# A graph network on one core: fixed places for the list's steps, PSUM places of their own for groups and dense blocks, and five count buffers

## The chip, the cores and the metric

The kernel runs on one core of one Trainium2 chip. The core has a matrix engine (PE, TensorE), a vector engine (DVE), a scalar engine (ACT), a general engine (POOL) and a queue engine (SP); each executes its own instructions strictly in order, and they wait for one another through semaphores. PE writes only into PSUM, which here is eight places ("banks") of 128 partitions x 2 KB, 512 float32 each. Everything else lies in SBUF (on the core) or DRAM, and DMA queues carry data between these.

The metric is device time in microseconds, median of the runs. The profile is one further execution, recorded by the hardware.

## The reference

The input is a graph of N = 12500 nodes with D = 256 features each and E = 200000 edges `src -> dst`, sorted by `dst`. The reference computes, first, three layers of mean aggregation, then a residual and a layer norm:

```
deg     = segment_sum(ones, dst)
inv_deg = 1 / max(deg, 1)
layer(h): agg = segment_sum(h[src], dst);  h @ W_self + (agg * inv_deg) @ W_neigh + b
h = relu(layer(x)); h = relu(layer(h)); h = layer(h)
x = layernorm(x + h)
```

and then an attention step over the same edges (4 heads of 16: scores of projected nodes, a softmax over each node's incoming edges, weighted sums, a few products with a 256 x 256 matrix), a residual and a layer norm. The attention step is not touched by the change.

## The kernel before

**Groups.** An aggregation is made as matrix products. 1792 edges (14 columns of 128) form a group. POOL gathers the sources' rows with 14 indirect DMAs (L121) into one of three buffers `xg`. DVE makes a one-hot of 128 x 1792 (L477, `oh`): for each edge, which of 128 consecutive nodes is its target; it compares the edges' relative targets with `nodes`, the numbers 0 to 127, which lie in a PSUM bank of their own (`gconst`, made at L471 by `group_consts`). PE multiplies the one-hot with the rows and sums in the bank `pA` (L906 in layer 1, L903 in layers 2 and 3), and carries over what the group before had begun (L486). In layers 2 and 3 a row is split in a high part (ACT, L895) and the low rest (DVE, L897), tile `hl` with two buffers of half a group; in layer 1 the rows go in as they are. Then a group's sums become means (ACT, L926), own rows `hb` and means are transposed on PE into `pT` (L384, function `turned`) and copied out to `hT` (DVE, L389); four products with the weights go into `pO` (L375, `sage_products`); DVE adds the bias in place (L365), ACT applies the relu (L367) and writes high parts (L682), DVE the low parts (`hs`, L684). In layer 3, DVE instead adds `x` (L369) and normalises, and `finish` transposes the result into `pT` once more (copied to `zT`, L389) and projects it into `pO` (L395, copied to `zu`, L397).

**Dense blocks.** The last 20 (layer 1) or 32 (layers 2 and 3) blocks of 128 nodes are not gathered. For these the kernel builds a table of counts, how often each node is a source for each target, as bytes in DRAM. A dense sweep goes over all 98 blocks of source nodes: it loads counts (`c8`) and rows in high and low parts (`hz`, three buffers in layers 2 and 3), casts the counts to float (`c32`, ACT, L772; five buffers in layer 1, three in layers 2 and 3), and sums on PE into `px` (L778; in layers 2 and 3 four banks, eight matmuls per source block). At a sweep's end its blocks pass through `end_block` (L723 on): the own rows `hbd` are transposed into `pT` (`hTd`, L389), products go into `pO` (L737) and, under the name pT, `pn` (L739), ACT copies one (`own`, L743), DVE joins both (L744), then come the same bias add and `finish`. All but the last sweep of a layer end in the banks `pT` and `pO` that the groups use; the last one ends in the `px` banks, through a small class `Spare`.

**The list.** In layer 1 the counts are formed besides: in eight parts of four blocks each. `row_ends` (L558 on) finds where each node's edges end, from a one-hot `oh16` made with the same `nodes` and summed by PE into `pO` (L563, read at L565). For each part, `load_edges` (L585 on) issues three loads on ACT's queue (`lim` L591, `prior` and `iv` L596), DVE turns them into first edges `org` and inverse degrees (L598 to L603), POOL gathers the sources and targets of these edges (`el`), and DVE makes keys of them (L613 to L630), which PE transposes (L634) and ACT copies (`kt`, L635). `form` then compares keys, four at a time (DVE, `oa` L656 and `ob` L657), PE multiplies the comparisons into `pc` (L665), ACT writes the counts (`win`, L668), and every finished block goes to DRAM (`cnt_d`, L673). The steps of the next part's `load_edges` are interleaved with `form` at fixed fractions of a part.

**PSUM.** The banks are `gconst`, `pT`, `pO` and `pA`, one each, and four for the rest: in layer 1 two `px` and two `pc`, in layers 2 and 3 four `px`.

**The order of the work.** The program is written as Python generators: per round three groups in different stages (late, far, now) take turns with units of a dense sweep and of the list. `chained` strings together PE's units (the first matmul of a unit behind the last of the unit before); `after` orders two instructions without a wait between engines. Apart from these, a scheduler places each instruction in its engine's order, by data and by a tile's buffers; two users of one PSUM bank are kept apart by waits.

Of the kernel before, what the change touches and what calls it, by code (L numbers as in the profile page):

```python
# [9 lines left out]
F32 = mybir.dt.float32  # L10
F32R = mybir.dt.float32r
# [6 lines left out]
OP = mybir.AluOpType  # L18
# [5 lines left out]
P = 128  # L24
# [24 lines left out]
def tile_gnn_resnorm(  # L49
# [341 lines left out]

    def project(ps, zT, zu):

        pz = ps.tile([zT.shape[2], KR], F32, name="pO")
        mm = [nc.tensor.matmul(pz, zT[:, c], uall[:, c].rearrange("p k r -> p (k r)"),  # L395
                               start=c == 0, stop=c == DC - 1) for c in range(DC)]
        return nc.vector.tensor_copy(zu, pz), mm[0], mm[-1]  # L397
# [90 lines left out]
    def fast_sage():  # L488
        with ExitStack() as fx:
# [11 lines left out]
            nc.vector.memset(top, 0.0)  # L501
            ones16 = wp.tile([P, 1], BF16, name="ones16")
            nc.vector.memset(ones16, 1.0)
            nodes = group_consts(cps)


            rows2 = rel.rearrange("p g j -> p (g j)")
# [50 lines left out]
            def row_ends(pool, g):  # L558

                oh = onehot(pool, nodes, mrel[:, g], BF16, "oh16", OP.is_le, 1)  # L560
                pn = ps.tile([1, P], F32, name="pO")
                for j in range(GT):
                    nc.tensor.matmul(pn, ones16, oh[:, j], start=j == 0, stop=j == GT - 1)  # L563
# [6 lines left out]
            held, whole, chain, closed, compared = [], [], [None], [None], [None]  # L570
            last = None

            def chained(first, last):
# [11 lines left out]
            def load_edges(pool, u):  # L585

                nonlocal last
                assert counted[0] >= needs[u]
                at = N0 + u * SG0 * P
                lim = pool.tile([P, 1], F32, name="lim")  # L590
                nc.scalar.dma_start(lim, ends_d[at - 1:at - 1 + SG0 * P, :].rearrange("(i t) o -> i (t o)", t=NC)[:, 0:1])  # L591

                iv = invd[:, u * SG0:(u + 1) * SG0]
                prior = pool.tile([P, SG0], F32, name="prior")
                for t, a in ((prior, at - 1), (iv, at)):
                    nc.scalar.dma_start(t, ends_d[a:a + SG0 * P, :].rearrange("(d p) o -> p (d o)", p=P))  # L596
                yield
                nc.vector.tensor_scalar_min(lim, lim, float(E - SL))  # L598
                org = pool.tile([P, 1], I32, name="org")
                nc.vector.tensor_copy(org, lim)  # L600
                nc.vector.tensor_sub(iv, iv, prior)
                nc.vector.tensor_scalar_max(iv, iv, 1.0)
                nc.vector.reciprocal(iv, iv)  # L603
                yield
                el = pool.tile([P, 2, SL], I32, name="el")
                for i, t in enumerate((sources, ends)):
                    i = gather(el[:, i], t, org)
                    if last is not None:
                        after(last, i)
                    last = i  # L610
                yield
                lead = pool.tile([P, 1], F32, name="lead")
                nc.vector.tensor_scalar(lead, pidx, float(NC), float(at), op0=OP.mult, op1=OP.add)  # L613
                part = pool.tile([P, 2, SL], I32, name="part")
                first = nc.vector.tensor_scalar(part[:, 0], el[:, 0], P - 1, None, op0=OP.bitwise_and)
                if compared[0] is not None:
                    after(compared[0], first)
                nc.vector.tensor_scalar(part[:, 1], el[:, 0], 7, None, op0=OP.logical_shift_right)
                keys = pool.tile([P, 4, SL], F32, name="keys")
                nc.vector.tensor_copy(keys[:, :2], part)  # L620

                node, odd, ok = keys[:, 3], keys[:, 2], part.bitcast(F32)[:, 0]
                nc.vector.tensor_scalar(node, el[:, 1], lead, None, op0=OP.subtract)
                nc.vector.tensor_scalar(odd, node, 2.0, None, op0=OP.is_ge)
                nc.vector.scalar_tensor_tensor(keys[:, 1], keys[:, 1], 2.0, odd, op0=OP.mult, op1=OP.add)
                nc.vector.scalar_tensor_tensor(odd, odd, -2.0, node, op0=OP.mult, op1=OP.add)
                nc.vector.tensor_scalar(odd, odd, 255.0, 1.0, op0=OP.mult, op1=OP.add)
                nc.vector.tensor_scalar(ok, node, 0.0, None, op0=OP.is_ge)
                nc.vector.scalar_tensor_tensor(ok, node, float(NC), ok, op0=OP.is_lt, op1=OP.mult)
                nc.vector.scalar_tensor_tensor(keys[:, 1], keys[:, 1], 1.0, ok, op0=OP.add, op1=OP.mult)  # L630
                kt = pool.tile([P, 3, P], F32, name="kt", bufs=2)
                pt = ps.tile([P, 3, P], F32, name="pT")
                for i in range(3):
                    nc.tensor.transpose(pt[:, i], keys[:, i], ident)  # L634
                nc.scalar.activation(kt, pt, AF.Copy)  # L635
                held.append(kt)

            def form(pool, psum):
# [6 lines left out]
                for i, u in enumerate(parts):  # L645
# [1 line left out]
                    kt = held.pop(0)  # L647
                    ahead = load_edges(pool, parts[i + 1]) if i + 1 < NU else iter(())
                    for i0 in range(0, P, CP):
                        if i0 in (0, P // 4, P // 4 * 3):  # L650
                            next(ahead, None)
                        oa = pool.tile([P, CP, P], BF16, name="oa", bufs=2)
                        ob = pool.tile([P, CP, NQ * 2], BF16, name="ob", bufs=2)
# [5 lines left out]
                        for c in range(0, CP, 2):  # L659
                            d = (i0 + c) * NC % P  # L660
                            if d == 0:
# [3 lines left out]
                            mm = [nc.tensor.matmul(pc[:, i].rearrange("p b t -> p (b t)"), oa[:, c + i], ob[:, c + i],  # L665
                                                   start=True, stop=True) for i in range(2)]
                            chained(*mm)
                            nc.scalar.activation(  # L668
                                win[:, :, d:d + 2 * NC].bitcast(U16).rearrange("p b (i t) -> p b i t", t=2),
                                pc.rearrange("p i b t -> p b i t"), AF.Copy)  # L670
                            if d + 2 * NC == P:
# [29 lines left out]
            class Spare:  # L701
# [3 lines left out]
                    self.pool, self.i = pool, i  # L705

                def tile(self, shape, dt, name):
                    return self.pool.tile(shape, dt, name=f"px{('pT', 'pO').index(name)}{self.i}")

            def sweeps(l, dk, dps, lk):  # L710

# [9 lines left out]
                def end_block(k, d, aggT, bank):  # L721
# [39 lines left out]
                for k0 in range(ND - NDL[l], ND, sg):  # L761
                    assert all(k in whole for k in range(k0, k0 + sg))
                    px = [[dps.tile([P, 512], F32, name=f"px{f}{i}") for i in range(sc // 512)] for f in range(DC)]
                    for b in range(NQ):
# [7 lines left out]
                        nc.scalar.activation(c32.rearrange("p (k d) -> p k d", d=P), c8[:, :, b % CB], AF.Copy)  # L772
                        made = []
                        for f in range(DC):
# [45 lines left out]
            for l in range(L):  # L820
# [6 lines left out]
                with ExitStack() as lx:  # L827
                    done, formed = 0, 0
                    lk = lx.enter_context(tc.tile_pool(name="layer", bufs=2))
                    dk = lx.enter_context(tc.tile_pool(name="dense", bufs=2))  # L830
                    dps = lx.enter_context(tc.tile_pool(name="dense_ps", bufs=1, space=PSUM))
                    steps_ = sweeps(l, dk, dps, lk)
                    if l == 0:
                        tk = lx.enter_context(tc.tile_pool(name="tabs", bufs=1))
# [4 lines left out]
                    def group(g):  # L839
# [40 lines left out]
                        pa = ps.tile([P, 2 * D], F32, name="pA")  # L880
                        for a in (0, H):
                            if a and final:
                                hT, *mm = turned(wk, ps, [hb], "hTd")
                                chained(*mm)
                                po = ps.tile([P, D], F32, name="pO")
# [63 lines left out]
                        store_rows(tiles, at[0], made, at[1])  # L949
# [369 lines left out]
```

## Time and profile before

| | us |
|---|---|
| median of 9 runs (lowest, highest) | 7903.2 (7852.78, 7944.66) |
| the profiled execution | 7867.0 |
| its span | 7865.2 |
| PE busy, share of the span | 5523.6, 70% |
| DVE busy | 3769.2, 48% |
| ACT busy | 3346.1, 43% |
| POOL busy | 4785.6, 61% |

The mean granted clock of PE is 0.776 of full speed. The profile's page lists the busy time of each engine, the busy share in 40 slices of the span, and the costliest groups of instructions; further views of the trace give the waits of an engine by what ended them, the same counts for a stretch of time, and single instructions in order of time. Layer 1 lies from the start to about 2080 us, layer 2 to 3765, layer 3 to 5550, and the attention step after that. In such lines "PE px L778 <- ACT c L772" means that PE stood idle before an instruction of line 778, which writes `px`, until ACT had finished one of line 772, which writes `c`; "issue" means that nothing in the trace shows what was waited for, "remote" that a signal from elsewhere came late, SPq, ACTq are DMA queues. Names in lines leave off figures at their end (`c` stands for `c32` and for `c8`).

### The profile page before, as it was taken

The page shows a single profiled execution, that of the slowest core. Times are in us where ns is not written, and L with a number is a line of the kernel's source. Part 1 is how long each engine was busy: PE and PEld are TensorE (multiplying, and loading weights), DVE is VectorE, ACT ScalarE, POOL GpSimd, SP SyncE. Part 2 cuts the span into 40 slices and gives each one's busy share as a digit, 9 for nine tenths or more (in the row PEclk, how much of TensorE's full clock was granted, in tenths as well). Part 3 has the DMA queues.
Part 4 walks back from the last instruction along what each step waited for, and adds up shares of the span by engine and source line. Part 5 has one row for each costly group of instructions (what it writes and reads, how often), then busy time and mean ns, then how long its engine had stood idle before and what let it go on. Part 6 is the DMA issues. An engine that isn't in the chain of part 4 may idle for free.

```text
span 7865.2 us, 85868 instructions
## 1 busy us (share of the span) xinstructions
PE 5523.6 (70%) x23570; PEld 4420.8 (56%) x23570; DVE 3769.2 (48%) x9563; ACT 3346.1 (43%) x6092; POOL 4785.6 (61%) x4977
## 2 busy tenths in 40 slices
PE   4688888788588888888688888877444444444445
PEld 3566666667466666666476667665343443343344
DVE  4555444444233444444344545545455555555555
ACT  1333333334154555554344445444344444444444
POOL 5566665566566566665565556556466666666665
PEclk6799999899789999999798989988555555555555
DMA  7767777677466666776576767665233322222322
GB/s 197 245 226 242 238 250 245 222 244 254 151 214 208 215 216 216 224 224 191 169 221 206 214 199 219 211 191 175 88 92 91 91 86 91 92 85 91 91 86 68
DMA packets 896848, 1391.60 MB, mean 177 GB/s; under 512 B 191296, under 2 KB 540504, under 8 KB 892253
## 3 DMA queue, kind: packets, MB, share of 16 engines
q1 hardware_dynamic: 654927, 834.75, 32.6%
q0 software_dynamic: 213152, 496.65, 21.5%
q10 hardware_dynamic: 28270, 54.56, 2.0%
q8 instruction: 189, 3.10, 0.2%
q14 instruction: 310, 2.54, 0.1%
HBM read 1175.15 MB, written 210.33 MB: 176 GB/s over the span
## 4 chain that ended last, share of the span: by engine, by line
PE 32%; issue 10%; DVE 9%; another core or an unknown queue 6%; POOL 6%; DMA 3%; ACT 2%; DVEq 0%; ACTq 0%; POOLq 0%; SPq 0%
PE px L778 11%; POOL zs L121 5%; PE pA L903 4%; PE pD L1050 3%; PE pA L1078 3%; PE pO L375 2%; DMA zs<-zu_d,srcI 2%; PE pO L402 2%; DVE zz L1058 2%; PE pO L408 2%; DVE hl L897 1%; DVE lg L1061 1%; PE pT L384 1%; DVE wf L1067 1%
## 5 line engine op out<-in xcount | busy, mean ns | idle before, releaser
L121 POOL DMA_INDIRECT xg<-h_d,srcI x2128 | 2074.1, 975 | 1397.4 <-issue 617.4
L778 PE MATMUL px<-c,hz 128*128 128x512 f32 x8232 | 2400.1, 431 | 233.6 <-issue 134.5
L121 POOL DMA_INDIRECT zs<-zu_d,srcI x1563 | 1492.7, 955 | 828.8 <-issue 416.9
L778 PEld LDWEIGHTS px<-c,hz 128*128 128x128 f32 x8232 | 1594.5, 202 | 595.5 <-issue 187.0
L772 ACT ACTIVATE c<-c 128x1024 fp32r<-128x1024 uint8 (+1 forms) x1274 | 1119.4, 891 | 1476.1 <-remote 500.4
L121 POOL DMA_INDIRECT xg<-in_x_dram,srcI x1218 | 1156.0, 949 | 776.2 <-PE pA L906 339.1
L477 DVE TENSOR_TENSOR oh<-rel,gconst 128x1792 fp32r<-128x1792 f32 (+1 forms) x354 | 713.5, 2016 | 1187.6 <-PE pO L408 390.2
L897 DVE TENSOR_TENSOR hl<-xg,hl 128x256 fp32r<-128x256 f32 x2128 | 776.0, 417 | 509.6 <-ACT hl L895 387.1
L1092 PE MATMUL pT<-ident,ag 128*64 128x128 f32 x112 | 47.2, 421 | 1159.1 <-DVE ag L418 749.7
L895 ACT ACTIVATE hl<-xg 128x512 fp32r<-128x512 f32 x1216 | 619.7, 568 | 297.0 <-PE pA L903 59.0
L906 PE MATMUL pA<-xg,oh 128*128 128x258 f32 x2520 | 669.6, 423 | 75.0 <-ACT agg L928 62.9
L1092 PEld LDWEIGHTS pT<-ident,ag 128*64 128x64 f32 x112 | 14.3, 128 | 1238.8 <-DVE ag L418 801.7
L903 PE MATMUL pA<-hl,oh 128*128 128x512 f32 x2128 | 600.4, 418 | 84.7 <-issue 75.9
L906 PEld LDWEIGHTS pA<-xg,oh 128*128 128x128 f32 x2520 | 535.2, 215 | 186.1 <-ACT agg L928 74.2
L903 PEld LDWEIGHTS pA<-hl,oh 128*128 128x128 f32 x2128 | 418.5, 199 | 189.7 <-issue 85.1
L668 ACT ACTIVATE win<-pc 128x392 uint16<-128x392 f32 x512 | 251.4, 496 | 628.2 <-remote 240.2
L1050 PE MATMUL pD<-z,ohT 128*128 128x128 f32 x1563 | 360.9, 418 | 54.6 <-DVE wf L1067 37.3
L1058 DVE TENSOR_TENSOR zz<-zs,pD 128x896 f32<-128x896 f32 x224 | 242.0, 1081 | 289.1 <-remote 136.7
L656 DVE TENSOR_SCALAR oa<-iota,kt 128x128 bf16<-128x128 f16 x1024 | 266.0, 260 | 238.0 <-PE pA L906 103.3
L365 DVE TENSOR_TENSOR pO<-b,pO 128x256 f32<-128x256 f32 x306 | 130.5, 426 | 519.4 <-remote 293.9
L1050 PEld LDWEIGHTS pD<-z,ohT 128*128 128x128 f32 x1563 | 346.9, 333 | 55.5 <-DVE wf L1067 31.5
L1078 PE MATMUL pA<-w,oh 128*128 128x136 f32 x1563 | 361.4, 418 | 0.0
(255 smaller groups left out, 7354.8 us busy)
## 6 DMA issues: line engine op xcount, KB each, us to landing
hz<-hs_d SPq DMA_DIRECT2D x637, 512.0 KB
c<-cnt_d SPq DMA_DIRECT2D x112, 896.0 KB
ohT<-rel_d SPq DMA_DIRECT2D x111, 896.0 KB
hs_d<-hs SPq DMA_DIRECT2D x218, 256.0 KB
cnt_d<-win ACTq DMA_DIRECT2D x32, 1568.0 KB
xg<-h_d,srcI POOLq DMA_INDIRECT x2128
c<-cnt_d SPq DMA_DIRECT2D x70, 448.0 KB
zs<-zu_d,srcI POOLq DMA_INDIRECT x1563
```

What stands on the lines that cost most here:

```text
L121: return nc.gpsimd.indirect_dma_start(out=dst_ap, out_offset=None, in_=table, in_offset=bass.IndirectOffsetOnAxis(ap=idx, axis=0))
L477: i = nc.vector.tensor_tensor(oh[:, :m], r[:, :m].unsqueeze(2).to_broadcast([P, m, P]), nodes.unsqueeze(1).to_broadcast([P, m, P]), op=op)
L656: nc.vector.tensor_scalar(oa[:, c], iota16[:, :P], kt[:, 0, at], None, op0=OP.is_equal)
L772: nc.scalar.activation(c32.rearrange("p (k d) -> p k d", d=P), c8[:, :, b % CB], AF.Copy)
L778: made.append(nc.tensor.matmul(px[f][i], hz[:, b % ZB, a:a + P].bitcast(F32R), c32[:, i * 512:(i + 1) * 512], start=b == 0 and part == 0, ...
L895: nc.scalar.activation(hi[:, j:j + n, :W], xg[:, a + j:a + j + n, :W], AF.Copy)
L897: nc.vector.tensor_tensor(lo[:, j, :D], xg[:, a + j, :D], hf[:, j, :D], op=OP.subtract)
L903: mm.append(nc.tensor.matmul(pa, oh[:, a + j], hl[:, j].rearrange("p i d -> p (i d)"), start=first, stop=stop))
L906: mm.append(nc.tensor.matmul(pa[:, :W], oh[:, a + j], xg[:, a + j, :W], start=first, stop=stop))
L1050: mm = [nc.tensor.matmul(pd[:, j * 2 * KR:(j + 1) * 2 * KR], ohT[:, a + j], z2.rearrange("p k i r -> p (k i r)"), start=True, stop=True) f ...
L1058: nc.vector.tensor_mul(zz, zg.unsqueeze(2).to_broadcast([P, n * K, 2, R]), pd[:, :n * 2 * KR].rearrange("p (m i r) -> p m i r", i=2, r=R))
L1078: mm = [nc.tensor.matmul(pa, oh[:, j], w[:, j], start=j == 0, stop=g == 0 and j == T - 1) for j in range(T)]
```

## The change

It has three parts.

1. **The list.** The three loads of a part now stand behind the last copy of counts (`win`, L668) that was written before them in the program; DVE's first steps on limits and on degrees (L598, L601), both steps on sources (L615, as before, and L618) and the first on targets (L623) behind the last comparison (`ob`, L657) written before them. The gathers of the first part are no longer strung together with the groups' gathers. The step on limits is taken at one half of a part, before at one quarter.
2. **PSUM.** One bank, `shared`, holds `nodes` in its first 128 columns. In layers 2 and 3 it also holds `pZ` of groups (64 columns), `pZ` of dense blocks (64 columns) and `pT` of dense blocks (256 columns); the bank `pO` is split into a left half for groups and a right half for dense blocks. The groups keep `pT` and `pA`. The projection, before in `pO`, goes into `pZ`. In layer 1 all stays as it was, but `pO` now belongs to the pool of the dense banks. A class `Places` gives out these slices by name.
3. **Count buffers.** `c32` has five buffers in layers 1 and 2 (before: five in layer 1 and three in layer 2) and three in layer 3, as before.

```diff
     def project(ps, zT, zu):
-        pz = ps.tile([zT.shape[2], KR], F32, name="pO")
+        pz = ps.tile([zT.shape[2], KR], F32, name="pZ")
...
-            nodes = group_consts(cps)
+            shared = cps.tile([P, 512], F32, name="shared")
+            nodes = shared[:, :P]
+            nc.vector.tensor_copy(nodes, iota)
+
+            class Places:
+                def __init__(self, pool, **places):
+                    self.pool, self.places = pool, places
+
+                def tile(self, shape, dt, name):
+                    if name not in self.places:
+                        pool = ps if name == "pT" else self.pool
+                        return pool.tile(shape, dt, name=name)
+                    t = self.places[name][:shape[0]]
+                    if len(shape) == 2:
+                        return t[:, :shape[1]]
+                    return t[:, :shape[1] * shape[2]].rearrange("p (a b) -> p a b", b=shape[2])
...
-                pn = ps.tile([1, P], F32, name="pO")
+                pn = beside.tile([1, P], F32, name="pO")
...
+                def behind(of, i):
+                    if of[0] is not None:
+                        after(of[0], i)
+                    return i
...
-                nc.scalar.dma_start(lim, ends_d[...])
+                behind(emptied, nc.scalar.dma_start(lim, ends_d[...]))
...
-                    nc.scalar.dma_start(t, ends_d[...])
+                    behind(emptied, nc.scalar.dma_start(t, ends_d[...]))
                 yield
-                nc.vector.tensor_scalar_min(lim, lim, float(E - SL))
+                behind(compared, nc.vector.tensor_scalar_min(lim, lim, float(E - SL)))
...
-                nc.vector.tensor_sub(iv, iv, prior)
+                behind(compared, nc.vector.tensor_sub(iv, iv, prior))
...
-                    if last is not None:
+                    if u != parts[0]:
                         after(last, i)
-                    last = i
+                        last = i
...
-                nc.vector.tensor_scalar(part[:, 1], el[:, 0], 7, None, op0=OP.logical_shift_right)
+                behind(compared, nc.vector.tensor_scalar(part[:, 1], el[:, 0], 7, None, op0=OP.logical_shift_right))
...
-                nc.vector.tensor_scalar(node, el[:, 1], lead, None, op0=OP.subtract)
+                behind(compared, nc.vector.tensor_scalar(node, el[:, 1], lead, None, op0=OP.subtract))
...
-                        if i0 in (0, P // 4, P // 4 * 3):
+                        if i0 in (0, P // 2, P // 4 * 3):
                             next(ahead, None)
...
-                            nc.scalar.activation(
+                            emptied[0] = nc.scalar.activation(
                                 win[...], pc.rearrange("p i b t -> p b i t"), AF.Copy)
...
-                    last = l == L - 1 and bank is not ps
+                    last = l == L - 1 and bank is not beside
...
-                        c32 = dk.tile([P, sc], F32R, name="c32", bufs=3 if l else 5)
+                        c32 = dk.tile([P, sc], F32R, name="c32", bufs=3 if l == L - 1 else 5)
...
-                    left = end_sweep(k0, aggT, [ps])
+                    left = end_sweep(k0, aggT, [beside])
...
+                    if l == 0:
+                        mine = beside = Places(dps)
+                    else:
+                        both = dps.tile([P, 2 * D], F32, name="pO")
+                        mine = Places(dps, pO=both[:, :D], pZ=shared[:, P:P + KR])
+                        beside = Places(dps, pO=both[:, D:], pZ=shared[:, P + KR:2 * P], pT=shared[:, 2 * P:])
...
-                            po, *mm = sage_products(ps, wts[l], hT)
+                            po, *mm = sage_products(mine, wts[l], hT)
...
-                        tiles, made = yield from finish(l, lk, ps, hn, po, light)
+                        tiles, made = yield from finish(l, lk, mine, hn, po, light)
```

(In the last group of layers 1 and 2, two more tiles are taken from `mine` instead of `ps`.)

More of the change, by code (lines that the diff above doesn't have):

```diff
@@ L569, in fast_sage @@
             sources, ends = src[:, None], dst[:, None]
-            held, whole, chain, closed, compared = [], [], [None], [None], [None]
+            held, whole, chain, closed, compared, emptied = [], [], [None], [None], [None], [None]
             last = None
@@ L590, in load_edges @@
                 lim = pool.tile([P, 1], F32, name="lim")
-                nc.scalar.dma_start(lim, ends_d[at - 1:at - 1 + SG0 * P, :].rearrange("(i t) o -> i (t o)", t=NC)[:, 0:1])
+                behind(emptied, nc.scalar.dma_start(
+                    lim, ends_d[at - 1:at - 1 + SG0 * P, :].rearrange("(i t) o -> i (t o)", t=NC)[:, 0:1]))
                 iv = invd[:, u * SG0:(u + 1) * SG0]
@@ L595, in load_edges @@
                 for t, a in ((prior, at - 1), (iv, at)):
-                    nc.scalar.dma_start(t, ends_d[a:a + SG0 * P, :].rearrange("(d p) o -> p (d o)", p=P))
+                    behind(emptied, nc.scalar.dma_start(t, ends_d[a:a + SG0 * P, :].rearrange("(d p) o -> p (d o)", p=P)))
                 yield
-                nc.vector.tensor_scalar_min(lim, lim, float(E - SL))
+                behind(compared, nc.vector.tensor_scalar_min(lim, lim, float(E - SL)))
                 org = pool.tile([P, 1], I32, name="org")
                 nc.vector.tensor_copy(org, lim)
-                nc.vector.tensor_sub(iv, iv, prior)
+                behind(compared, nc.vector.tensor_sub(iv, iv, prior))
                 nc.vector.tensor_scalar_max(iv, iv, 1.0)
@@ L614, in load_edges @@
                 part = pool.tile([P, 2, SL], I32, name="part")
[L615 to L618, printed above, removed]
+                behind(compared, nc.vector.tensor_scalar(part[:, 0], el[:, 0], P - 1, None, op0=OP.bitwise_and))
+                behind(compared, nc.vector.tensor_scalar(part[:, 1], el[:, 0], 7, None, op0=OP.logical_shift_right))
                 keys = pool.tile([P, 4, SL], F32, name="keys")
@@ L707, in tile @@
                 def tile(self, shape, dt, name):
-                    return self.pool.tile(shape, dt, name=f"px{('pT', 'pO').index(name)}{self.i}")
+                    return self.pool.tile(shape, dt, name=f"px{int(name != 'pT')}{self.i}")
             def sweeps(l, dk, dps, lk):
@@ L882, in group @@
                             if a and final:
-                                hT, *mm = turned(wk, ps, [hb], "hTd")
+                                hT, *mm = turned(wk, mine, [hb], "hTd")
                                 chained(*mm)
-                                po = ps.tile([P, D], F32, name="pO")
+                                po = mine.tile([P, D], F32, name="pO")
                                 mm = [nc.tensor.matmul(po, hT[:, c], wts[l][0][:, c], start=c == 0, stop=False)
```

## The prediction

> **What bounds the kernel now.** I began with the page's busy times (PE 70% of the span, POOL 61%, DVE 48%, ACT 43%), then cut the span at the layers' borders with the windows view (start and end; then length and the busy time of PE, its weight loads, DVE, ACT and POOL; the granted clock; the DMA share; GB/s):
>
> ```profile
> 0.00:2080.00 2080.00, 1611.90 (x7593) 1268.11 (x7593) 976.45 (x3185) 714.21 (x1556) 1218.81 (x1286) 0.88 0.72 232
> 2080.00:3765.00 1685.00, 1386.03 (x5614) 1089.15 (x5614) 713.15 (x1657) 820.42 (x1416) 1032.87 (x1064) 0.90 0.66 209
> 3765.00:5550.00 1785.00, 1437.77 (x6210) 1151.59 (x6210) 893.10 (x2464) 819.18 (x1441) 1041.22 (x1064) 0.89 0.65 198
> 5550.00:7865.00 2315.00, 1087.88 (x4153) 911.98 (x4153) 1186.55 (x2260) 992.29 (x1681) 1492.69 (x1563) 0.50 0.29 88
> ```
>
> PE sets the three layers (77%, 82% and 81% busy), idle 468, 299 and 347 us. The last 2315 us are attention, which the change leaves alone. So the change is worth what it takes from, or adds to, those idle times. Which waits they are, the waits of PE say (time in all, times, longest), for layer 2 (the first four lines) and layer 3:
>
> ```profile
> PE px L778 <- ACT c L772: 52.9, 24, 17.2
> ...
> PE pT L384 <- DVE hTd L389: 11.9, 5, 4.3
> ...
> PE pT L384 <- DVE pO L744: 7.8, 4, 2.3
> ...
> PE pT L384 <- DVE hT L389: 1.4, 2, 0.8
> ...
> PE pT L384 <- DVE zT L389: 60.2, 15, 7.6
> ...
> PE pT L384 <- DVE hTd L389: 35.0, 10, 9.6
> ...
> PE pO L375 <- DVE zu L397: 24.3, 5, 11.4
> ...
> PE pT L384 <- DVE pO L744: 11.0, 5, 7.2
> ...
> PE pT L384 <- DVE hT L389: 6.4, 4, 2.5
> ```
>
> To see: a transpose or product that waits on a copy out of PSUM, because groups and dense blocks share one pT and one pO. In layer 1 the change touches a wait of DVE, which the waits before line 618 show:
>
> ```profile
>   DMA el<-in_src_dram,org: 31.6, 5
>   issue: 7.5, 1
> ```
>
> **The sum** is made against the profiled execution, 7867.0 us (span 7865.2, 1.8 us around it), 36 us under the runs' median of 7903.2 and inside them (7852.78 to 7944.66); I add its result to the median. About 0.3%, 24 us, is what can be told from no change.
>
> **Layer 1, the list: -19 us.** Eight times (once per part) the list's step issues three DMAs on ACT's queue, five DVE operations for the limits, two gathers on POOL and twelve DVE operations for the keys. None is added or removed. What moves is their place, as the order of the two built programs tells. L618 (0.23 us) is in before free to stand before its data: at 530.2, 750.7 and four later places DVE stands until the gather of `el` has landed, and behind it stand the compares that feed pc, the bias add of a finished group, and through that hs and the row ends:
>
> ```profile
> 530.24 0.23 DVE L618 TENSOR_SCALAR part<-el 128x128 int32<-128x128 int32 x1 [6.45 <-DMA el<-in_src_dram,org]
> 530.39 0.42 DVE L365 TENSOR_TENSOR pO<-b,pO 128x256 f32<-128x256 f32 x1
> ...
> 532.01 1.65 PE L563 MATMUL pO<-oh,ones 128*1 128x128 bf16 x14 [4.06 <-DVE hs L684]
> ```
>
> Behind the part's last compare the data have been there for over 90 us. PE's gaps beside the six places are 4.1, 1.9, 7.9, 6.0, 4.1 and 4.3 us, 28 in all; 16.5% of such time PE would idle anyway, so 23 go. In return some six more operations of about 0.23 us (L618, L623, L624 and what follows them) come at each of seven part ends, just ahead of the transposes that the next part's counts wait for: at most 10 us, of which 4 taken, as PE has groups to work on. The limits' DMAs move up to 336 us later on ACT's queue (the last part's from 1200.9 to 1537.2), still over 85 us before their reader; the gathers on POOL keep their order. POOL waits at the first part only, 17 us (its `org` is made at 314.6, its gather stood at 297.6), and has 339 us of waits for PE's sums in this layer to take that from. Bounds: -45 (all 39 us of DVE's stand and 6 of waits for the limits) to +10.
>
> **Layer 2, five count buffers: -27 us.** PE waits 52.9 us for a cast, of which 17.2 is the layer's start and stays. The other 23 waits are 1.55 us each. Two more buffers let ACT run two units ahead, 2 x 8 matmuls x 0.227 = 3.6 us, more than such a wait. I take three quarters of 35.7; the rest are casts that come late for another reason. Bounds -36 to 0. A loss is excluded on this side: ACT is 49% busy, and casts move ahead of the rows' high parts, whose low parts PE waited for 0.6 us in the layer.
>
> **Layers 2 and 3, places of their own: -33 us.** The waits shown come to 21.1 us in layer 2 (hTd, L744, hT) and 76.7 in layer 3 (hTd, zu, L744, hT); nearly all of these pairs are gone from the built program. That of zT (60.2) mostly stays, since the groups' zT and next hT keep one pT. I count a third. These long waits fall where PE's signals came late to everybody, and PE, let through, soon meets its next reader:
>
> ```profile
> 4137.18 0.42 DVE L389 COPY zT<-pT 128x256 f32<-128x256 f32 x1 [10.44 <-remote]
> 4137.20 1.06 ACT L772 ACTIVATE c<-c 128x1024 fp32r<-128x1024 uint8 x1 [12.36 <-remote]
> ...
> 4137.66 0.69 PE L384 MATMUL pT<-ident,hb 128*128 128x128 f32 x2 [7.18 <-DVE zT L389]
> ```
>
> Here DVE and ACT stand 10 and 12 us for the same cause, and no place in PSUM cures that. Bounds: -98 (all) to 0. The pairs of pO's two halves still wait on one another, being one bank.
>
> **The same layers, the one-hot: +46 us.** `nodes` now lies in the bank that dense blocks transpose and sum in, and every one-hot (2.02 us, L477) reads it. In before it runs about a whole group ahead:
>
> ```profile
> 2628.62 2.02 DVE L477 TENSOR_TENSOR oh<-rel,gconst 128x1792 fp32r<-128x1792 f32 x1 [3.12 <-PE pA L903]
> ...
> 2661.79 0.38 PE L384 MATMUL pT<-ident,hbd 128*128 128x128 f32 x2
> ...
> 2661.93 1.89 PE L903 MATMUL pA<-hl,oh 128*128 128x512 f32 x7
> ...
> 2665.05 0.42 DVE L389 COPY hTd<-pT 128x256 f32<-128x256 f32 x1 [5.10 <-PE pA L903]
> ```
>
> (made at 2628.62, used at 2661.93). In the built order of after it stands behind hTd, L744 or zu out of that bank, about one group's low parts (L897) later, and the first matmul of pA waits on it in 61 of 152 groups, in before in none. Behind it on DVE are the next low parts, and behind pA on PE everything. In these 61 the work between the transposes and pA is some 12 px matmuls, 12 x 0.227 = 2.72 us; needed are a copy of 0.42 or 0.49, 2.02 and 0.1 for handing over: 2.6. In layer 2 (25 groups) that just holds. In layer 3 (36) a zT copy of 0.42 and a statistics step of 0.17 often lie between: 0.45 us short, 16 us. A copy that meets a busy DVE (half the time, half of 0.42) adds 0.1 to each, 6 us. And each is one more step of the kind of pT <- zT, which costs 60.2 us over layer 3's 76 groups, 0.79 each: 48 over 61, of which I take half, 24, since some fall in waits that PE has anyway. Bounds: 0 (hidden as before) to 61 x 2.47 = 151 (no cover).
>
> The Trainium skill, "PSUM — Partial Sum Buffer", section "PSUM bank collisions raise a hardware error", says that accesses are to be kept apart by bank and quadrant, not by address, and that a bank is 2 KiB. That speaks against this change: four places in one bank are one resource. By addresses alone the one-hot would cost nothing and the time would be 7824; by the rule it is the 7870 below. The trace of before shows no such sharing.
>
> **Sum:** -19 - 27 - 33 + 46 = -33; 7867 becomes 7834, the median 7903 about **7870**.
>
> **Rivals.**
> 1. The one-hot becomes the wait of the layers. Against -79 of gains it costs 61 times x: even at x = 1.3 us, slower by over 0.3% from 1.7, and at the full 2.47 +72, 7975. For it: the hTd copy above started 2.9 us after its transposes ended (2662.17). Against it: DVE stood there behind the one-hot's own wait for pA, which after has behind the copy.
> 2. The cured waits only move to the next late signal, casts included, and only the list and the one-hot's 16 us count: -3, 7900, no change. For it: the 10 to 12 us of "remote" above.
> 3. The waits go whole: -35 (39 less 4) - 36 - 98 + 22 = -147, 7756. Against it: the same lines.
> 4. The change doesn't do what it says, as halves of one bank are still taken in turn: the 33 shrink to the 15 or so that pT's move alone gives, 7888.
>
> **How the numbers follow.** The likeliest, the sum with its own range of 7840 to 7895, 0.42 (0.30 faster, 0.12 same); rival 1, 0.32, slower; rivals 2 and 4 together 0.15 (0.12 same, 0.03 faster); rival 3, 0.11, faster. Together 0.44, 0.24, 0.32. The range of 7790 to 7965 cuts half of rival 3 and the far end of rival 1.
>
> **What would show it.** List: L618's waits for `el` fall from 39 us to nearly none, layer 1 ends some 20 us sooner. Buffers: px <- c in layer 2 near 26 us. Places: PE's waits for hTd, zu and L744 shrink in layer 3, those for zT stay. One-hot: a line pA L903 <- oh L477 appears, 30 to 60 us in layers 2 and 3; over 100 there and I am wrong towards slower. If those two layers are longer though it is small, ACT's new order (casts ahead of high parts) would be the culprit, and I would have missed it.

## The result and the profile after

The changed kernel takes 7989.0 us (median) against 7901.0 for the kernel before in the same comparison: ratio 1.0111, 95% interval 1.0094 to 1.0128. It is 1.1% slower, where 7870 had been forecast, and past the upper end of the range. Rival 1, the one-hot as the layers' new wait, had 7975. The profiled execution of after is 7989.0 us, its span 7987.0.

One thing must be said first, since ratios can't be understood without it. The later runs came in five series, each on another chip (the expectations say "call" for a series), and met two surroundings. In the first series, as in the two profiles compared here, many waits are ended by "remote" (DVE alone stands some 910 us so in before); there the kernel before takes 7830 us. In the other four series no wait is ended so, and the same kernel takes 6480 us. Every ratio is to the kernel before within one series. I write "late signals" for the first kind.

Cut at the last pA of each layer, the three layers and the attention of after read (length, busy time of PE, its weight loads, DVE, ACT, POOL; granted clock, DMA share, GB/s):

```profile
0.00:2044.60 2044.60, 1601.59 (x7584) 1259.50 (x7585) 972.77 (x3180) 715.43 (x1556) 1220.94 (x1286) 0.89 0.73 236
2044.60:3816.10 1771.50, 1398.65 (x5615) 1105.93 (x5614) 717.61 (x1656) 820.65 (x1412) 1038.85 (x1064) 0.87 0.63 198
3816.10:5666.30 1850.20, 1467.53 (x6200) 1158.42 (x6200) 905.30 (x2462) 820.31 (x1440) 1037.78 (x1064) 0.88 0.63 192
5666.30:7987.00 2320.70, 1091.88 (x4175) 915.10 (x4173) 1188.20 (x2265) 993.73 (x1685) 1495.03 (x1563) 0.50 0.29 88
```

| cut at the last pA, us | before | after | difference |
|---|---|---|---|
| layer 1 | 2075.8 | 2044.6 | -31 |
| layer 2 | 1683.5 | 1771.5 | +88 |
| layer 3 | 1786.2 | 1850.2 | +64 |
| attention | 2319.7 | 2320.7 | +1 |

So the loss is in layers 2 and 3, 152 us. Cut the same way, PE is busy 1386.0 and 1436.4 us in these layers of before, idle 647 in all; in after it is idle 755. That is 108 of the 152. The other 44 are the same matmuls taking longer: PE's busy time went from 2822 to 2866 us, while the granted clock fell from 0.90 and 0.89 to 0.87 and 0.88. It is pA's matmuls that take longer, 715 us in place of 667.

The waits of PE in after, layer 2 and then layer 3 (us in all, times, longest):

```profile
PE pA L931 <- DVE oh L477: 109.7, 17, 9.3
...
PE pA L931 <- DVE oh L477: 46.1, 14, 5.0
PE pO L759 <- DVE y L369: 37.6, 4, 11.7
PE pO L375 <- DVE y L369: 37.3, 6, 11.5
PE pT L384 <- DVE zT L389: 22.6, 7, 5.8
...
PE shared L384 <- DVE zu L397: 3.8, 1, 3.8
```

The waits of pT for hTd and L744 are gone, as the change means to. zu's are not cured so well: pO no longer waits for zu (24.3 us in before), and the shared bank waits 3.8 us for it, but pO now waits for y, the step before zu: the groups' products 37.3 us, where before had no such line, and the dense blocks' 37.6 (24.9 in before). Besides these stands a wait that the two layers of before did not have: the first matmul of pA waits 31 times for the one-hot, 155.8 us. One of the 31 in order of time:

```profile
3198.54 0.38 PE L384 MATMUL shared<-ident,hbd 128*128 128x128 f32 x2
...
3200.50 1.17 PE L800 MATMUL px<-c,hz 128*128 128x512 f32 x4
...
3208.48 0.42 DVE L389 COPY hTd<-shared 128x256 f32<-128x256 f32 x1 [11.11 <-remote]
...
3208.82 2.01 DVE L477 TENSOR_TENSOR oh<-rel,shared 128x1792 fp32r<-128x1792 f32 x1
...
3210.97 2.47 PE L931 MATMUL pA<-hl,oh 128*128 128x512 f32 x5 [9.30 <-DVE oh L477]
```

To see: PE has transposed by 3198.92 and does its cover (other work that it has before pA, here px matmuls) until 3201.67. The copy out of the shared bank starts only at 3208.48, after a wait ended by "remote"; the one-hot can't pass it, and pA stands 9.3 us. Ten of the 17 waits in layer 2 are 8.2 to 9.3 us long. In layer 2 only dense blocks use the shared bank besides `nodes`, and each of the 17 one-hots starts directly behind DVE's read of their places in it (hTd 9 times, L766, which was L744, 8 times). Just ahead of each of the ten long ones stands a wait ended by "remote", of DVE itself or of ACT, which copies `own` for L766.

The matmuls behind such a stand are slow too. For the 9.2 us of this stand and for the 3.33 us behind it the windows view has (the granted clock is the third figure from the end)

```profile
3201.70:3210.90 9.20, 0.00 (x0) 0.00 (x0) 2.42 (x3) 2.11 (x2) 3.32 (x4) 0.67 0.63 194
3210.97:3214.30 3.33, 3.33 (x8) 2.65 (x9) 0.46 (x1) 0.00 (x0) 0.00 (x0) 0.50 0.01 2
```

so pA's first seven matmuls take 3.32 us, where 1.80 is usual in these layers (the median). Over the 31 waits that comes to some 35 us, most of the 44.

### The profile page after: what moved, and what is told of

It reads as the page before. It is cut to its first block, busy times and chain, and to the rows that moved or that the text cites. A ratio compares the mean times of both kernels' runs of the same rounds, so it can differ in the third digit from the quotient of the medians.

```text
span 7987.0 us, 85767 instructions
## 1 busy us (share of the span) xinstructions
PE 5559.7 (70%) x23570; PEld 4438.9 (56%) x23570; DVE 3783.9 (47%) x9563; ACT 3350.1 (42%) x6092; POOL 4792.6 (60%) x4977
## 5 line engine op out<-in xcount | busy, mean ns | idle before, releaser
L931 PE MATMUL pA<-hl,oh 128*128 128x512 f32 x2128 | 645.9, 442 | 290.1 <-DVE oh L477 155.8
L931 PEld LDWEIGHTS pA<-hl,oh 128*128 128x128 f32 x2128 | 440.3, 211 | 428.8 <-issue 244.7
L477 DVE TENSOR_TENSOR oh<-rel,shared 128x1792 fp32r<-128x1792 f32 (+1 forms) x242 | 486.8, 2012 | 318.9 <-remote 114.7
L477 DVE TENSOR_TENSOR oh<-rel,gconst 128x1792 fp32r<-128x1792 f32 x112 | 225.6, 2015 | 649.4 <-PE pO L408 415.9
```

What stands on the lines that cost most here:

```text
L477: i = nc.vector.tensor_tensor(oh[:, :m], r[:, :m].unsqueeze(2).to_broadcast([P, m, P]), nodes.unsqueeze(1).to_broadcast([P, m, P]), op=op)
L931: mm.append(nc.tensor.matmul(pa, oh[:, a + j], hl[:, j].rearrange("p i d -> p (i d)"), start=first, stop=stop))
```

## The experiments

### In a series with late signals

**Numbers from SBUF.** The changed kernel, with one edit:

```diff
-            nodes = shared[:, :P]
-            nc.vector.tensor_copy(nodes, iota)
+            nodes = iota
```

> The changed kernel, but the numbers 0 to 127 that the one-hots compare with are read from SBUF (iota), so that the one-hots no longer touch the shared bank; all places stay. Theory (the one-hot is kept behind the dense blocks' and projections' use of its bank): the wait of pA for oh, 156 us in layers 2 and 3 of the changed kernel, falls under 15 us; layer 2 (from layer 1's last pA to its own last pA) falls from 1771 us to 1690 or less, layer 3 from 1850 to 1800 or less; total 7830 to 7880 against about 7900 before and 7989 changed, if a one-hot from SBUF also takes about 2.02 us. Rival (ACT's new order, casts ahead of high parts, made layers 2 and 3 long): both stay within 20 us of 1771 and 1850, total 7970 to 8000.

Measured: 7774.6 us, ratio 0.9913 (0.9880 to 0.9945). Layers 1 to 3 are 2057, 1678 and 1737 us, and no wait of pA for oh is left in layers 2 and 3. The absolute total of the forecast missed, since this series' kernel before was at 7830 and not at 7900; layers 2 and 3 are as the theory had them, and the rival's 1771 and 1850 are out. Late signals were not fewer here: DVE stands 1349 us for "remote" in this profile, 919 in after's. A one-hot from SBUF takes 2.02 us as well. But the gathers on POOL became slower (second and third columns: busy time, mean ns of one):

```profile
L121 POOL DMA_INDIRECT xg<-h_d,srcI x2128 | 2271.9, 1068 | 1143.8 <-issue 467.5 <-remote 135.6 <-DMA hs_d<-hs 91.6
...
L121 POOL DMA_INDIRECT xg<-in_x_dram,srcI x1218 | 1306.1, 1072 | 618.2 <-issue 251.2 <-PE pA L933 186.7 <-remote 62.0
```

1068 and 1072 ns, against 976 and 951 in after. POOL still idles here (1143.8 us ahead of the first kind), and what the slower gathers cost in this series no run separates.

**Three count buffers again.** The changed kernel with `bufs=3 if l else 5`.

> The changed kernel with three count buffers in layer 2 as before. Theory (shared bank): total within 25 us of 7989, layer 2 at 1760 to 1800 us with pA's wait for oh still near 110. Rival (the two more buffers let casts push the rows' high parts back): layer 2 returns to about 1690, total to about 7905.

Measured: 7921.9 us, ratio 1.0114 (1.0069 to 1.0159), as the change's own 1.0111. In its profile pA waits 65.6 us for oh in layer 2, where near 110 was expected, and 41.8 in layer 3; layer 2 takes 1747 us, less than the theory's 1760 and far from the rival's 1690. The buffers, and ACT's new order with them, are not the loss.

**The list alone.** The kernel before, with only the changes to `load_edges` and `form`.

> The kernel before with the list's new places alone. Theory (DVE no longer stands at the shift for the gather of el): L1 to its last pA 2045 us against 2076, DVE's wait for el under 3 us against 39, layers 2 and 3 as before; total 7870, ratio 0.996. Rival (the 31 us by which layer 1 was shorter in the one profile of the changed kernel are scatter between executions, or come from pO's bank moving to another pool): within 10 us of the kernel before.

Measured: 7828.2 us, ratio 0.9996 (0.9969 to 1.0022). DVE's waits for `el` are gone from the profile; layer 1 is at 2059 us in that profile, where the theory had 2045 against 2076, but the whole is no faster. The theory's effect was there, and its gain can't be told from nothing, as the rival had it.

**List and buffers.** The same and, besides, `bufs=3 if l == L - 1 else 5`.

> The kernel before with the list's new places and five count buffers in layer 2, no PSUM places. Forecast's step: another 27 us (bounds 0 to 36) below the list alone, layer 2 at about 1657 us, wait of px for casts there near 26 us against 53; total about 7845. Rival (the cured waits move on to the next late signal): layer 2 within 8 us of 1684, total as the list alone, 7870.

Measured: 7812.3 us, ratio 0.9983 (0.9954 to 1.0011): 0.13% below the list alone, with intervals of 0.28% on either side. Layer 2 takes 1709 us in its one profile, against 1680 in that of the list alone: longer than the forecast's 1657 and also than the rival's 1684 with its 8 us. PE's waits in layer 2, of the list alone,

```profile
PE px L789 <- ACT c L783: 48.0, 25, 10.6
...
PE pO L748 <- DVE hs L695: 27.4, 5, 7.2
...
PE pO L375 <- DVE hs L695: 14.3, 5, 8.5
...
PE pT L750 <- DVE hT L389: 3.7, 3, 2.2
```

and of list and buffers:

```profile
PE pO L748 <- DVE hs L695: 41.2, 8, 10.2
...
PE pT L750 <- DVE hT L389: 28.3, 5, 12.2
PE pO L375 <- DVE hs L695: 27.3, 4, 10.1
```

The 48 us for casts are gone to the last; 51 more stand before hs and hT. A cured wait became another one.

### In series without late signals

**The kernel before, once more.**

> The kernel before once more, for its stages on the chip and in the call of the next three runs. Layers as in its first profile if a stage is steady between executions: 2076, 1684 and 1786 us (to the last pA of each), each within 15 us; more scatter than that would mean that a difference of 30 us in one stage of one profile shows nothing.

Measured: 6485.6 us, layers 1679, 1391 and 1382 us. The expectation is void: this was the first sight of the second kind of surroundings. Its layers, as above:

```profile
0.00:1679.20 1679.20, 1487.08 (x7585) 1199.02 (x7586) 969.93 (x3180) 729.16 (x1555) 1222.99 (x1286) 0.94 0.87 287
1679.20:3069.80 1390.60, 1288.30 (x5616) 1047.76 (x5615) 726.60 (x1656) 837.58 (x1412) 1036.59 (x1064) 0.96 0.79 252
3069.80:4451.70 1381.90, 1326.40 (x6199) 1088.82 (x6198) 902.97 (x2462) 826.82 (x1440) 1037.05 (x1064) 0.98 0.83 257
```

Layers 2 and 3 leave PE idle 158 us, where the profile that I forecast from left it 647. Most of the idle time that I had set out to price is there only with late signals.

**The places alone.** The change without its list and without its buffers, in three series.

> The kernel before with the PSUM places alone (nodes in the shared bank; old list, three count buffers). Theory (the one-hot behind its bank's other users): all of the loss, ratio 1.010 to 1.016, pA's wait for oh 90 to 160 us in layers 2 and 3 together. Rival (the loss needs the three parts together, or is the list's): ratio 1.000 to 1.005.

> The PSUM places alone again. Theory (late signals): ratio 1.010 to 1.018 where the trace shows remote waits, and 1.000 as in the last call (11 us of pA's wait for oh) where it shows none. Rival (the places alone cost nothing, it needs five buffers or the new list beside them): 0.998 to 1.004 with remote waits too.

> The PSUM places alone, for a call with late signals: ratio 1.010 to 1.018 and pA's wait for oh over 90 us by the theory, 0.998 to 1.004 by the rival that the loss needs the buffers or the list; without late signals 1.000 again.

Measured: 1.0002 (0.9993 to 1.0012), 1.0006 (0.9997 to 1.0016) and 0.9997 (0.9987 to 1.0006), with 8 to 11 us of pA's wait for oh. The same tight place, in the third:

```profile
2421.84 0.38 PE L384 MATMUL shared<-ident,hbd 128*128 128x128 f32 x2
...
2422.26 0.42 DVE L389 COPY hTd<-shared 128x256 f32<-128x256 f32 x1 [1.25 <-PE shared L384]
...
2422.60 2.01 DVE L477 TENSOR_TENSOR oh<-rel,shared 128x1792 fp32r<-128x1792 f32 x1
...
2424.81 1.81 PE L926 MATMUL pA<-hl,oh 128*128 128x512 f32 x7
```

The transposes end at 2422.22, the copy starts 0.04 us later, the one-hot is done at 2424.61, and pA starts at 2424.81 without a wait: the cover of 12 px matmuls just holds. The first expectation (a loss in any case) failed; those of the second and third, for series without late signals, held.

**The change itself, again.**

> The changed kernel once more, beside the next three. Theory (PE's signals that reach DVE 10 us late turn the one-hot's tight place into waits): where the trace shows waits ended by remote (some 2000 us over all engines in the first profile of the kernel before), ratio 1.008 to 1.014 and pA's wait for oh over 100 us; where it shows none, as in the last call, that wait is under 20 us, and the list's gain is all that is left, ratio 0.992 to 0.997. Rival (the one-hot's place costs by itself, whatever the signals do): over 60 us of pA's wait for oh in both.

Measured: 6448.8 us, ratio 0.9934 (0.9917 to 0.9950), with 7.4 us of that wait. The very change that loses 1.1% with late signals gains 0.7% without them. Its gain lies in layer 1 (1634 us against 1679).

**The list alone, again**, to see whose gain that is.

> The list's new places alone, again. Theory (DVE's stand at the shift is a real cost, which late signals cover up): without late signals layer 1 at 1635 us against 1679, ratio 0.993 to 0.995; with them 0.997 to 1.002 as in the first call. Rival (the 40 us in layer 1 came from pO's moving to the dense banks' pool): 0.999 to 1.001 without late signals.

Measured: 6423.1 us, ratio 0.9919 (0.9902 to 0.9935), layer 1 at 1626 us: it is the list's, and more than expected. What stood before the shift in the kernel before (its waits, from the run above):

```profile
  DMA el<-in_src_dram,org: 89.6, 6
```

Without late signals DVE comes to the shift sooner and stands longer for the same gather, 90 us in place of 32, and layer 1 gets 53 us back. It is the safest of these kernels: no slower with late signals (0.9996), and here at least as fast as the whole change. The version with the numbers in SBUF is faster with late signals (0.9913), but what those numbers cost without them comes next but one.

**The dense blocks' pT back with the groups'.** The changed kernel with:

```diff
-beside = Places(dps, pO=both[:, D:], pZ=shared[:, P + KR:2 * P], pT=shared[:, 2 * P:])
+beside = Places(dps, pO=both[:, D:], pZ=shared[:, P + KR:2 * P])
```

It was to show how much of the loss hangs on that one place; in the built program pA waits on the one-hot directly in 10 groups in place of 61.

> The changed kernel, but dense blocks transpose and sum in the groups' pT again; the shared bank holds nodes and the two projections, which only layer 3 has. Theory: layer 2 has no other user of the bank left, so its wait of pA for oh goes from 110 us to under 5 and the layer to 1700 or less; layer 3, where zu is still in the bank, keeps a part of its 46 us and gets the waits of pT for hTd back (some 20 to 35 us), 1770 to 1830; ratio 1.000 to 1.006. Rival (the place of pZ and pO matters, not the dense blocks' pT): layer 2 stays at 1750 or more, ratio 1.010 or more.

> The changed kernel with the dense blocks' pT back in the groups' bank, again. Theory (late signals at the tight place): with remote waits, layer 2 has no wait of pA for oh over 5 us and comes to within 30 us of the kernel before, layer 3 keeps some (zu still in the bank), ratio 0.998 to 1.006; without them 0.9936 as in the last call. Rival (pZ and the split pO bring the loss): 1.008 or more with remote waits.

> The changed kernel with the dense blocks' pT in the groups' bank, for a call with late signals: by the theory ratio 0.998 to 1.006, layer 2 without a wait of pA for oh; by the rival (pZ's and pO's places) 1.008 or more; without late signals 0.994 again.

> The changed kernel with the dense blocks' pT back in the groups' bank. Theory (one-hot in the dense blocks' bank): with late signals ratio 0.998 to 1.006 and no wait of pA for oh in layer 2; rival (pZ's and pO's places) 1.008 or more. Without late signals 0.994, as twice before.

Measured: 0.9936, 0.9943, 0.9936 and 0.9934 (intervals of 0.0015 to 0.0017 on either side), all without late signals, where there was nothing to undo. Its ratio with late signals was never measured. What speaks for the place is the trace of after alone: in layer 2 all 17 waits stand behind a read of the dense blocks' places.

**Places with the numbers from SBUF, without list and buffers.**

> The same, but nodes read from SBUF. Theory: the loss turns into the gain of the places, ratio 0.990 to 0.996, as list and buffers gave nothing that could be told (0.9996 and 0.9983); waits of pT for hTd, zu and L744's pO nearly gone in layers 2 and 3. Rival (the gain of 0.991 with nodes in SBUF came from list and buffers, which can pay only with the new places): 0.998 to 1.002.

> The PSUM places alone with the numbers read from SBUF, again. A gather on POOL took 1060 to 1083 ns beside one-hots from SBUF against 950 to 975 beside those from PSUM. Theory (POOL pays for the one-hot's reads, and that only counts where PE leaves POOL no slack): ratio 1.047 as in the last call without remote waits; with them, where POOL idles some 1000 us more, 0.990 to 1.000. Rival (the places with nodes in SBUF are faster only through the list's or the buffers' part, of which the run of 0.9913 had both): 1.01 or more with remote waits too.

Measured: 1.0471 (1.0457 to 1.0485) and 1.0468 (1.0450 to 1.0485). I had expected a gain in the first; the second confirms the loss. In the second run a gather takes POOL 1086 and 1059 ns,

```profile
L121 POOL DMA_INDIRECT xg<-h_d,srcI x2128 | 2254.2, 1059 | 688.0 <-issue 309.1 <-DVE hl L919 130.7 <-DMA xg<-h_d,srcI 68.2
...
L121 POOL DMA_INDIRECT xg<-in_x_dram,srcI x1218 | 1322.8, 1086 | 379.5 <-issue 139.2 <-PE pA L928 113.2 <-PE pc L681 38.7
```

and with the one-hots from PSUM, in the places alone of the same series:

```profile
L121 POOL DMA_INDIRECT xg<-h_d,srcI x2128 | 2075.1, 975 | 700.8 <-issue 298.8 <-DVE hl L920 131.3 <-DMA xg<-h_d,srcI 77.1
...
L121 POOL DMA_INDIRECT xg<-in_x_dram,srcI x1218 | 1156.7, 950 | 397.6 <-PE pA L929 131.4 <-issue 117.6 <-PE pc L682 51.3
```

That is 179 + 166 = 345 us more POOL time, and the kernel is 300 us longer. The attention step's gathers, beside one-hots that read PSUM in both kernels, take 958 and 957 ns. Without late signals POOL has no slack to give: in layers 2 and 3 of the places alone it stands only 0.3 us between two gathers, whatever ends the wait,

```profile
POOL xg L121 <- issue: 293.1, 962, 0.3
POOL xg L121 <- DVE hl L920: 129.2, 424, 0.3
```

and the only longer stand is one of 25.3 us.

**Every one-hot made twice**, in the kernel before and in the places alone, to make it late by a means of my own:

```diff
+                        if l:
+                            nc.vector.tensor_tensor(oh, srel.unsqueeze(2).to_broadcast([P, GT, P]),
+                                                    nodes.unsqueeze(1).to_broadcast([P, GT, P]), op=OP.is_equal)
```

> The kernel before with every one-hot of layers 2 and 3 made twice (the same values, 2.02 us more on DVE for each of 152 groups, 307 us of DVE's time in all): what a late one-hot costs where it is a whole group ahead. Theory (the place in DVE's order decides): pA's wait for oh stays under 5 us; loss only by DVE's load, ratio 1.000 to 1.010. Rival (any 2 us more in front of low parts and copies cost as much, wherever they stand): 1.02 or more.

> The PSUM places alone, with every one-hot of layers 2 and 3 made twice. Theory: in the 61 tight groups the second one-hot is without cover, up to 61 x 2.02 = 123 us more for PE, so at least 60 us over the places alone and over twice_before: ratio 1.010 to 1.03 without late signals, 1.02 to 1.05 with them; pA's wait for oh 60 us or more. Rival (what made the loss is another place): as twice_before, within 0.4%.

Measured: 1.0012 (1.0002 to 1.0021) for the kernel before, 1.0032 (1.0019 to 1.0044) for the places, whose pA waits 23.0 us for oh, twice_before's none in these layers. The sign is the theory's, the size (60 us and more) is not, and the rival's 0.4% holds. The scheduler knows the second one-hot and puts more PE work before pA: in the built programs 16 to 26 px matmuls (18 at the median) stand between the shared bank's transposes and the first pA of such a group, against 9 to 16 (12) in the places alone. A delay that the scheduler plans for is not the delay that the first series had, so this pair decides little.

## Why the prediction was wrong

**What bounds the kernel:** right as to PE. But the idle time was read as belonging to the steps that the waits name, and 489 us of the 647 in layers 2 and 3 go away without late signals and without any edit.

**Layer 1, the list, -19.** Right in mechanism: L618's stand is gone wherever the list has its new places (2.9 us at most is left). With late signals it measured -3 us (0.9996; -24 to +17), so -19 lies inside and can't be told from nothing; without, -52 (0.9919). That layer 1 was 31 us shorter in the one profile of after may be the list or scatter; the runs don't separate these.

**Five count buffers, -27.** The waits went, as told; the time did not (-10 from the list alone to list and buffers, inside the intervals). Here rival 2 was the better account: in the two profiles they moved to hs and hT. The sentence that a wait of 1.55 us is covered by 3.6 us of lead was true, and not the question.

**Places, -33.** The waits for hTd and L744 went; pO's for zu went too, but the forecast counted its 24.3 us as curable, and in after pO waits 37.3 us for y in its place. The worth of the places, one-hot apart, is the step from list and buffers (0.9983) to the numbers in SBUF (0.9913): -55 us, with some 33 on either side, and in spite of slower gathers. So the size was about right, perhaps a little low.

**The one-hot, +46: this step failed.** Its mechanism was there: `shared`, the copy, the one-hot behind it, pA waiting, 61 tight groups. The static part was not too small either: without late signals the places alone show 8 to 11 us of that wait, where I had 16, and 6 for a busy DVE. The failing part is the price of lateness. I took 0.79 us a time from pT <- zT, and half of it, 24 us in all, "since some fall in waits that PE has anyway". Neither step was sound. The 0.79 spread 15 waits of 4.0 us over 76 groups, while 31 of the 61 tight groups (those whose pA waits on the one-hot directly) waited, 5.0 us each and up to 9.3; and that row gave no reason to halve, since DVE's zT copies stood 72.2 us for "remote" and PE stood 60.2 us for them. Measured, for the +46: 155.8 us of waits, and by ratios 147 us, with some 53 on either side (from 1.0114 less 0.9996 for the places with the shared bank, 92 us, and the 55 that they would have gained). The named bound, 61 x 2.47 = 151, met that figure by chance: it was the price of a missing cover in all 61 groups. How late a signal comes was no part of it.

**The rule of the Trainium skill** ("PSUM — Partial Sum Buffer", "PSUM bank collisions raise a hardware error"), that accesses are kept apart by bank and quadrant and not by address, led to the row that decided. This program's waits follow the bank: 31 waits in the trace of after, and none in layers 2 and 3 with the numbers elsewhere; by addresses alone I had 7824. What the chip does with accesses that nothing keeps apart, no run here shows.

**What would have been right:** I had shown in the forecast itself that DVE's copies start 10 us late on a "remote" signal, and used it only to mark down the gains. The same lines priced the loss: a step that comes behind such a copy with 2.7 us of cover for a need of 2.6 waits for nearly all that the signal is late (in the lines of after above the copy starts 9.56 us after its transposes, and pA stands 9.30). How often it happens stood in the waits of DVE in before, layers 2 and 3:

```profile
DVE pO L365 <- remote: 239.8, 29, 11.5
...
DVE zT L389 <- remote: 72.2, 12, 10.7
```

These and five more such lines come to 67 waits and 471 us over 152 groups, 7.0 us each. My estimate after the fact: at that rate 61 tight groups meet 27 of them, 189 us, and rival 1 has the greater chance.

## What to carry to other kernels

- Cover counts by its slack, not by its length. A scheduler that places a matmul where its model has the operand just ready leaves none, and then a late signal is paid nearly in full. Look for the operands that used to be a whole stage ahead and no longer are.
- Before a wait is priced, see what ended it. A wait that ends late for everybody isn't the named step's, and curing it moves it.
- Constants that every stage reads don't belong in a bank that one stage writes, nor where reading them slows another engine: in PSUM the one-hot's numbers cost order, in SBUF they cost POOL's gathers.

## What the runs showed of the hardware

- **Late signals.** The same kernel took 7830 us in one series and 6480 in four others, each on another chip. With late signals, waits ended by "remote" are some 910 us on DVE alone and PE's granted clock is 0.776; without, none and 0.816. What makes them, and whether it belongs to a chip or to a time, no run here shows.
- **A one-hot from SBUF slows POOL's gathers**, from 950 and 975 ns to 1086 and 1059, while itself it takes 2.02 us from either place. The Trainium skill, "SBUF — State Buffer", section "Who interferes with whom", has it that a DVE instruction with both inputs in SBUF contends with a GpSimd instruction that reads SBUF. These rows agree, though they don't show which access contends. 345 us over 282 such one-hots (40 of them for the row ends) are 1.2 us for each.
- **The clock follows the waits:** behind a stand of PE of 9.3 us the granted clock is 0.50, and seven matmuls of pA take 3.32 us in place of 1.80. Of the 152 us lost in layers 2 and 3, 44 are slower matmuls, not idle time.
